# Moving the copy of a tile's attention sums from the next tile's first task to the place directly behind the sums

## The chip, the cores and the metric

The kernel runs on one core of a Trainium2 chip. The metric is device time in microseconds (us) of one execution, as the median of several runs. A core has a matrix engine (PE, with its weight loads PEld), a vector engine (DVE), a scalar engine (ACT), a general engine (POOL) and a queue engine that issues transfers (SP). Each works through its own list of instructions in order, and they wait for each other by semaphores.

## What is computed

The input is x of shape 2 x 2048 x 256 in float32, that is 4096 rows or 32 tiles of 128 rows. Two layers follow each other, each a product of two branches:

```
xn = layernorm(x)
x1 = x  + attention_L0(xn) * silu(experts_L0(xn))     # first layer
xn = layernorm(x1)
out = x1 + block_L1(xn) * silu(two_layer_block(xn))   # block_L1: the main branch
```

attention_L0 has 16 heads with a window of 128 rows, plus a "latent" attention over means of 32 rows, and a sigmoid gate per head that mixes the two. experts_L0 sends every row to one of eight experts. block_L1 is a layer norm, attention in buckets of 64 rows that see their own and the previous bucket, an output projection, and a GELU feed-forward. The two-layer block (local attention with 8 heads, a gated feed-forward, twice) lies between the two and isn't touched here.

For both attentions the part that matters is the same. For a tile n with two blocks of 64 rows: scores, softmax weights without the division, weights times values (the sums), then sums divided by the weights' totals, turned, and multiplied by the output matrix.

## The kernel before, in words

There are three stages in time. The first layer (attention and experts together) takes about the first 980 us, the two-layer block runs from there to about 2490 us, and the main branch runs from there to the end at 3112 us.

**A tile of attention.** Tile n has the runs 2n and 2n+1, one for each block of 64 rows. In the first layer a run has these tasks. `turn(i, half)` transposes two of the four weight tiles on PE (line 151) and copies them out of PSUM (`pt`, line 69 on ACT or line 71 on DVE, in turn). `small(i)` turns the second half, issues the scores of run i+2 (line 114 on PE, then eight masked minima on DVE at line 107 and eight exponentials on ACT at line 136) and then the sums of run i (`total`, 24 matmuls at line 165 into two PSUM banks called `acc`). In the main branch `turn_weights(i)` turns all four weight tiles (line 1502), and `small(i)` issues the scores of run i+2 (lines 1469, 107 and 1489) and the sums of run i (16 matmuls at line 165).

**What follows a tile's second run.** `finish(n)` returns the steps that end tile n. Its first step is `take`: it copies the two `acc` banks into `aT` in SBUF, one copy on DVE (line 71) and one on ACT (line 69), and inverts the weights' totals `zs` on DVE (lines 860 and 861 in the first layer, line 1522 in the main branch). `divide` transposes `aT` on PE (line 188) and multiplies by the inverse totals on DVE (line 192). In the first layer `weigh`, `gate` and `mix` follow (lines 870 to 883, on POOL, DVE and ACT). `back` transposes the result (line 252) and copies it to `oT` on ACT (line 254), and `out` multiplies by the output matrix (line 261) and adds on DVE (line 890 or 1534).

**The order is written out by hand.** `attention(g)` builds a list (a lane) of pairs of a weight and a step for the four tiles of a group. `in_turn` gives each step of a lane a place by the middle of its weight in the lane's sum, stretches the lane over a given part of the group's time, and issues the steps of all lanes in the order of these places. Other lanes are `head(g+1)` (projections of the next group), `experts()`, the sending of rows to the experts (32 indirect transfers at line 547 on POOL) and, in the main branch, `forward(g)` (the feed-forward, lines 1585 to 1619). The step `none` does nothing and only holds a place. All engines keep the order of issue.

In this order tile n-1's `finish` is spread over tile n: `take` comes right after tile n's first task (`first`, the turning of run 2n), `divide` somewhat later, still ahead of `small(2n)`.

**Buffers.** The `acc` banks come from a pool of two. All other PSUM tiles (`s` for products, `tp` for transposes) share six banks. `aT` has two buffers, `zs` three.

Of the kernel before, what the change touches and what calls it, by code (L numbers as in the profile page):

```python
# [14 lines left out]
NT = B * S // P  # L15
# [3 lines left out]
NG = NT // GT  # L19
# [11 lines left out]
def kernel(ctx: ExitStack, tc: tile.TileContext, io: dict, col: dict):  # L31
# [4 lines left out]
    def sb(pool, shape, tag, bufs=None):  # L36
        kw = {} if bufs is None else {"bufs": bufs}
        return pool.tile(list(shape), F32, name=tag, tag=tag, **kw)
# [4 lines left out]
    def bank(tag):  # L43
        return ps.tile([P, 512], F32, name=tag, tag="acc" if tag == "acc" else "b", bufs=2 if tag == "acc" else 6)
# [45 lines left out]
    def in_turn(*lanes):  # L90

        order = []
        for i, (a, b, lane) in enumerate(lanes):
            total, at = sum(w for w, _ in lane), 0.0
            for w, do in lane:
                order.append((a + (b - a) * (at + w / 2) / total, i, len(order), do))
                at += w
        for _, _, _, do in sorted(order, key=lambda x: x[:3]):
            do()
# [279 lines left out]
    with ExitStack() as l0_ctx, tc.manual_schedule(engines=ordered):  # L379
# [264 lines left out]
            return lane  # L644


        groups, values, zss, accs, scores, turns, outs = {}, {}, {}, {}, {}, {}, {}

        def head(g):

# [163 lines left out]
        def latent_out(n):  # L814

            d = outs[n] = {}

            def take():

                d["latT"] = sb(pa, [64, 2, 64], "latT")  # L820
                for v in range(2):
                    h = slice(32 * v, 32 * v + 32)
                    lat = d["latT"][h]
                    acc = accs[n][v][h, 2:4, :].rearrange("p b (e q) -> p b e q", e=2)
                    first, second = (cols[h, col[name] : col[name] + 1] for name in ("first", "second"))
                    nc.scalar.activation(lat, acc[:, :, 0, :], AF.Copy, scale=first)
                    nc.vector.scalar_tensor_tensor(lat, acc[:, :, 1, :], second, lat, ALU.mult, ALU.add)

            def spread():
                mm = bank("s")  # L830
                for blk in range(2):
                    for e in range(2):
                        nc.tensor.matmul(
                            mm[64 * e : 64 * e + 64, blk * P : (blk + 1) * P],
                            lhsT=d["latT"][:, blk, :],
                            rhs=routw[:, e, :],
                            start=True,
                            stop=True,
                        )
                rem = d["rem"] = sb(pa, [P, 16, 16], "rem")  # L840
                nc.vector.tensor_tensor(
                    rem.rearrange("p (b h) d -> p b (h d)", b=2),
                    mm[:, 0 : 2 * P].rearrange("p (b n) -> p b n", b=2),
                    bc(brout, 1, [P, 2, P]),
                    ALU.add,
                )
                d["g2"] = sb(pa, [P, 16, 16], "g2")
                nc.gpsimd.tensor_tensor(d["g2"], rem, bc(gr, 1, [P, 16, 16]), ALU.mult)

            return take, spread  # L850

        def finish(n):

            d = outs[n]

            def take():
                acc = accs.pop(n)
                d["aT"] = sums_out(pa, acc)
                zs = zss[n]
                nc.vector.tensor_scalar(zs, zs, 1e-30, None, ALU.max)  # L860
                nc.vector.reciprocal(zs, zs)

            def divide():
                d["o"] = divided(pa, d["aT"], zss.pop(n))

            lo = lambda: d["o"].rearrange("p b v s d -> p (b v s) d")

            def weigh():
                d["g1"] = sb(pa, [P, 16, 16], "g1")
                nc.gpsimd.tensor_tensor(d["g1"], lo(), bc(gl, 1, [P, 16, 16]), ALU.mult)  # L870
                nc.gpsimd.tensor_tensor(d["g1"], d["g1"], d["g2"], ALU.add)
                nc.gpsimd.tensor_tensor(lo(), lo(), d["rem"], ALU.subtract)

            def gate():
                d["gate"] = sb(pa, [P, 16], "gate")
                nc.vector.tensor_reduce(d["gate"], d["g1"], AX.X, ALU.add)
                nc.scalar.activation(d["gate"], d["gate"], AF.Exp, scale=-1.0)

            def mix():
                nc.vector.tensor_scalar(d["gate"], d["gate"], 1.0, None, ALU.add)  # L880
                nc.vector.reciprocal(d["gate"], d["gate"])
                nc.vector.tensor_tensor(lo(), lo(), bc(d["gate"], 2, [P, 16, 16]), ALU.mult)
                nc.gpsimd.tensor_tensor(lo(), lo(), d["rem"], ALU.add)

            def back():
                d["oT"] = turned_out(pa, d["o"].rearrange("p b v s d -> p b (v s d)"))

            def out():
                s = sb(pa, [P, D], "s")
                nc.vector.tensor_tensor(s, times_out(d["oT"], outw), bout, ALU.add)  # L890
                nc.sync.dma_start(rows_s[:, n, :], s)
                del outs[n]

            return [take, divide, weigh, gate, mix, back, out]

        def attention(g):

            lane = []
            none = lambda: None
            for n in range(GT * g, GT * (g + 1)):  # L900
                take, divide, weigh, gate, mix, back, out = finish(n - 1) if n else [none] * 7
                take_latent, spread = latent_out(n)
                ahead = [none] * 3
                if n + 1 < NT:
                    ahead = [lambda f=f, n=n: f(n + 1) for f in (scale_latent, turn_latent, project_values)]
                def small(i, before):

                    turn(i, 1)
                    for f in before:
                        f()  # L910
                    if i + 2 < 2 * NT:
                        score(i + 2)
                    total(i)

                first, second = (lambda i=i: turn(i, 0) for i in (2 * n, 2 * n + 1))
                latent = [lambda n=n: total_latent(n), take_latent]
                lane += [(1, first), (0.5, take), (1.2, none), (0.8, divide), (0.3, weigh), (0.5, none)]
                lane += [(2.4, lambda n=n, latent=latent: small(2 * n, latent)), (0.3, gate), (1, none), (0.6, spread), (2, none)]
                lane += [(1, second), (0.3, ahead[0]), (0.3, mix), (1.7, none)]
                lane += [(2.4, lambda n=n: small(2 * n + 1, [])), (0.7, none), (0.6, ahead[2]), (0.7, none)]  # L920
                lane += [(0.4, back), (0.7, none), (0.3, ahead[1]), (0.7, none), (0.5, out), (0.5, none)]
            return lane

# [10 lines left out]
        for g in range(NG):  # L934
# [20 lines left out]
                (_, fetch), *rest = gate_head(0)  # L955
                lanes += [(0.3, 0.4, [(1, fetch)]), (0.77, 1, rest)]
            in_turn(*lanes)
        for step in finish(NT - 1):
            step()

    wd = ctx.enter_context(tc.tile_pool(name="wd", bufs=1, side="left"))
# [5 lines left out]
    with tc.tile_pool(name="pd", bufs=2, side="left") as pd, tc.manual_schedule(engines=ordered):  # L967
# [81 lines left out]
        x1s, tiles, scores, turns, accs, outs = {}, {}, {}, {}, {}, {}  # L1049
# [298 lines left out]
        for r in range(NR):  # L1348
            lanes.append((r, r + 1, attention(r)))
            ahead = [prepare(m) for m in range(GT * r + 2, min(GT * r + GT + 2, NM))]  # L1350
# [27 lines left out]
    with tc.tile_pool(name="pc", bufs=2, side="left") as pc, tc.manual_schedule(engines=ordered):  # L1378
# [5 lines left out]
        zero_v = sb(pc, [P, 2, P], "zero_v", 1)  # L1384
        nc.vector.memset(zero_v, 0.0)
        yout = io["out"].rearrange("b (n p) d -> p (b n) d", p=P)
        groups, values, zss, accs, scores, turns, outs = {}, {}, {}, {}, {}, {}, {}

        def head(g):

# [149 lines left out]
        def attention(g):  # L1540

            lane = []
            none = lambda: None
            for n in range(GT * g, GT * (g + 1)):
                take, divide, back, out = finish(n - 1) if n else [none] * 4
                ahead = (lambda n=n: project_values(n + 1)) if n + 1 < NT else none

                def small(i):

                    if i + 2 < 2 * NT:  # L1550
                        score(i + 2)
                    total(i)

                first, second = (lambda i=i: turn_weights(i) for i in (2 * n, 2 * n + 1))
                lane += [(1, first), (0.3, take), (1.2, none), (0.7, divide), (0.6, none)]
                lane += [(1.2, lambda n=n: small(2 * n)), (1.8, none), (0.5, back), (1, none)]
                lane += [(1, second), (2, none)]
                lane += [(1.2, lambda n=n: small(2 * n + 1)), (0.8, none), (0.5, out), (0.8, none), (1, ahead), (0.6, none)]
            return lane

        def forward(g, t0=0, nt=GT):
# [79 lines left out]
        lanes += [(NG - 1.73, NG - 0.6, forward(NG - 3)), (NG - 0.73, NG - 0.25, forward(NG - 2))]  # L1641
        lanes.append((NG - 0.24, NG, forward(NG - 1, 0, 2)))
        in_turn(*lanes)
        in_turn((0, 0.6, [(1, step) for step in finish(NT - 1)]), (0, 1, forward(NG - 1, 2, 1)))
        in_turn((0, 1, forward(NG - 1, 3, 1)))


# [142 lines left out]
```

## Time and profile before

| quantity | value |
|---|---|
| median of 3 runs | 3109.21 us (3105.69 to 3111.13) |
| the profiled execution's own time | 3114.02 us |
| its span, first to last instruction | 3112.2 us |
| granted TensorE clock, mean | 0.947 |
| PE busy | 2757.3 us, 89% |
| DVE busy | 1885.1 us, 61% |
| ACT busy | 1676.9 us, 54% |
| POOL busy | 1064.6 us, 34% |
| instructions | 72624 |
| `aT` copies, DVE and ACT | 64 each, median 378 ns |
| transposes of `aT` (line 188) | 256, median 273 ns |

The page lists busy time for each engine, the span in 40 slices, the chain of work that ended last and the costliest groups of instructions. Other views list one line's or one tile's instructions with what their engine waited for, instructions in order of time, and sums over windows of time. In a row of the timeline the columns are the start and the length in us, engine, line, operation, what it writes and reads, and the count. A matmul in float32 appears twice in the trace for each one in the program. A bracket at the end gives the time that the engine sat idle before the instruction, and who released it.

### The profile page before, as it was taken

How to read it: one execution, taken by the hardware profiler on the slowest of the kernel's cores; microseconds unless marked ns; L12 is line 12 of the kernel's file. 1: busy time of each engine (PE TensorE's matmuls, PEld its weight loads, DVE VectorE, ACT ScalarE, POOL GpSimd, SP SyncE). 2: the span in 40 equal slices, each digit the busy share in tenths (PEclk: the TensorE clock that was granted, in tenths of full speed). 3: DMA queues.
4: the chain of work that ended last, by engine and by line, in shares of the span. 5: the costliest groups of instructions: out<-in, count | busy, mean ns of one | idle time of the engine just before them, and what ended most of it. 6: DMA issues, size and time to landing. Idle time of an engine off the chain costs nothing.

```text
span 3112.2 us, 72624 instructions
## 1 busy us (share of the span) xinstructions
PE 2757.3 (89%) x28250; PEld 1980.8 (64%) x28250; DVE 1885.1 (61%) x6708; ACT 1676.9 (54%) x4598; POOL 1064.6 (34%) x1227
## 2 busy tenths in 40 slices
PE   7776899999994789999999999999998689999997
PEld 4554778877872556665666666666665556666666
DVE  5765555545563777777676676666665375555542
ACT  4544667767771344444544445455553277667662
POOL 1224233323234555454443444443441112222212
PEclk8888999999996899999999999999999899999998
DMA  5001422222212001110000010000000100000000
GB/s 170 13 22 59 142 98 91 94 86 91 98 63 88 26 25 28 28 28 25 15 18 29 15 37 8 8 8 5 5 2 16 57 9 25 22 24 23 15 15 21
DMA packets 88417, 128.63 MB, mean 41 GB/s; under 512 B 8173, under 2 KB 78220, under 8 KB 83084
## 3 DMA queue, kind: packets, MB, share of 16 engines
q1 hardware_dynamic: 85004, 115.60, 11.6%
q0 software_dynamic: 3072, 8.39, 0.8%
q8 instruction: 225, 3.69, 0.5%
q14 instruction: 116, 0.95, 0.1%
HBM read 88.58 MB, written 27.00 MB: 37 GB/s over the span
## 4 chain that ended last, share of the span: by engine, by line
PE 32%; DVE 6%; issue 4%; POOL 4%; ACT 4%; DMA 0%; SPq 0%; POOLq 0%; DVEq 0%; ACTq 0%
PE s L1296 7%; PE s L1612 3%; PE s L1599 3%; PE s L1318 3%; PE s L1086 3%; ACT pr L1489 2%; PE s L1214 2%; POOL inv L1130 1%; PE s L1102 1%; PE acc L1041 1%; POOL scr L1119 1%; PE s L1011 1%; PE tp L151 1%; PE tp L1502 1%; PE s L1469 1%
## 5 line engine op out<-in xcount | busy, mean ns | idle before, releaser
L1031 ACT ACTIVATE pr<-pr,mn 128x192 f32<-128x192 f32 (+2 forms) x512 | 188.6, 439 | 275.8 <-DVE mn L107 271.7
L1130 POOL TENSOR_TENSOR inv<-inv,nhalf 128x16 f32<-128x16 f32 x64 | 188.4, 2944 | 413.6 <-DVE inv L1129 413.6
L107 DVE CUSTOM_DVE_ANT_0 pr<-s,cst 128x128 f32<-128x128 f32 (+2 forms) x1024 | 261.5, 316 | 101.7 <-PE s L1469 81.0
L1296 PE MATMUL s<-h2T,d_w 128*128 128x512 f32 (+2 forms) x792 | 317.0, 555 | 0.6 <-DVE h2T L1286 0.6
L69 ACT COPY pt<-tp 128x384 f32<-128x384 f32 (+3 forms) x320 | 156.3, 495 | 270.9 <-PE tp L151 249.7
L151 PE MATMUL tp<-cst,pr 128*128 128x128 f32 x1488 | 220.3, 285 | 60.5 <-ACT pr L1031 52.0
L136 ACT ACTIVATE pr<-pr,mn 128x192 f32<-128x192 f32 (+2 forms) x512 | 222.9, 436 | 67.4 <-DVE mn L107 67.0
L1489 ACT ACTIVATE pr<-pr,mn 128x128 f32<-128x128 f32 x512 | 198.1, 388 | 112.7 <-DVE mn L107 112.4
L151 PEld LDWEIGHTS tp<-cst,pr 128*128 128x128 f32 x1488 | 180.4, 147 | 102.3 <-ACT pr L1031 57.8
L1119 POOL TENSOR_TENSOR scr<-scr,tab 128x512 f32<-128x512 f32 x128 | 176.8, 1381 | 200.6 <-DVE scr L71 200.5
L1086 PE MATMUL s<-d_wqkv,hT 128*128 128x512 f32 x512 | 243.1, 618 | 0.0
L1296 PEld LDWEIGHTS s<-h2T,d_w 128*128 128x128 f32 x792 | 146.0, 198 | 141.6 <-issue 135.4
L71 DVE COPY pt<-tp 128x384 f32<-128x384 f32 (+3 forms) x320 | 181.3, 567 | 72.0 <-PE tp L151 53.4
L1309 DVE SCALAR_TENSOR_TENSOR u<-s,cols,ge 128x512 f32<-128x512 f32 (+2 forms) x108 | 74.0, 689 | 201.6 <-PE s L1296 130.6
L1318 PE MATMUL s<-d_w,u 128*128 128x256 f32 x768 | 177.9, 382 | 0.0
L165 PE MATMUL acc<-pt,v 64*32 64x128 f32 x4992 | 124.3, 291 | 40.8 <-DVE pt L71 28.5
L1086 PEld LDWEIGHTS s<-d_wqkv,hT 128*128 128x128 f32 x512 | 97.6, 201 | 98.4 <-issue 97.6
L611 PE MATMUL s<-Wo,it 128*128 128x128 f32 x1248 | 158.3, 281 | 1.6 <-ACT it L603 0.8
L1617 POOL TENSOR_TENSOR y<-y,stream 128x256 f32<-128x256 f32 x32 | 23.3, 728 | 391.9 <-DVE y L1616 391.9
L1318 PEld LDWEIGHTS s<-d_w,u 128*128 128x128 f32 x768 | 142.5, 190 | 22.5 <-issue 3.1
L611 PEld LDWEIGHTS s<-Wo,it 128*128 128x128 f32 x1248 | 149.1, 195 | 10.2 <-issue 7.1
L107 DVE CUSTOM_DVE_ANT_0 pr<-s,cst_a 128x192 f32<-128x192 f32 (+2 forms) x512 | 144.0, 347 | 9.3 <-PE s L114 6.9
(271 smaller groups left out, 6416.8 us busy)
## 6 DMA issues: line engine op xcount, KB each, us to landing
w<-in_W1b_dram SPq DMA_DIRECT2D x39, 1028.0 KB
xsort<-zero SPq DMA_DIRECT2D x1, 4992.0 KB
xs<-xsort SPq DMA_DIRECT2D x39, 128.0 KB
ysort<-ys SPq DMA_DIRECT2D x39, 128.0 KB
xn<-in_L_attn_x_dram SPq DMA_DIRECT2D x8, 512.0 KB
rows_s<-s SPq DMA_DIRECT2D x32, 128.0 KB
stream<-in_L_attn_x_dram SPq DMA_DIRECT2D x8, 512.0 KB
sg<-rows_s SPq DMA_DIRECT2D x8, 512.0 KB
```

Of the source, the lines that this page charges most:

```text
L71: nc.vector.tensor_copy(out, in_)
L107: nc.vector.tensor_tensor_reduce(pr, sc, mask, 1.0, CAP, ALU.add, ALU.min, mn)
L136: nc.scalar.activation(w, w, AF.Exp, bias=mn[:, v : v + 1], scale=-1.0, accum_out=zs[:, v, blk, s : s + 1])
L151: nc.tensor.transpose(tp[:, k * P : (k + 1) * P], pr[:, k, :, :].rearrange("p v j -> p (v j)"), ident)
L611: nc.tensor.matmul(mm, lhsT=d["it"][:, ic, :], rhs=late["Wo"][:, ic, h], start=(ic == 0), stop=(ic == FF // P - 1))
L1031: nc.scalar.activation(p, p, AF.Exp, bias=mn[:, w : w + 1], scale=-1.0)
L1086: nc.tensor.matmul(mm, lhsT=heads[r][:, k, t * P : (t + 1) * P], rhs=wqkv_d[l][:, k, j * INNER : (j + 1) * INNER], start=(k == 0), stop=(k ...
L1119: nc.gpsimd.tensor_tensor(d["r2"][:, :, :, 32 * hf : 32 * hf + 32], d["qk"][:, :, :, 32 - 32 * hf : 64 - 32 * hf], bc(d["tab"][:, 2:4, hf, ...
L1130: nc.gpsimd.tensor_tensor(inv.rearrange("p a h -> p (a h)"), inv.rearrange("p a h -> p (a h)"), nhalf, ALU.pow)
L1296: nc.tensor.matmul(mm, lhsT=w1[l][:, k, c, :], rhs=d["h2T"][:, k, 0:w], start=(k == 0), stop=(k == 1))
L1318: nc.tensor.matmul(mm[:, 0:D], lhsT=d["u"][:, c, i * P : (i + 1) * P], rhs=w2[l][:, c, :], start=(c == 0), stop=(c == HC - 1),)
L1489: nc.scalar.activation(w, w, AF.Exp, bias=mn[:, v : v + 1], scale=-1.0, accum_out=zs[:, v, blk, st : st + 1])
```

## The change

In the first layer and in the main branch, `take` of tile n moves from behind `first` of tile n+1 to behind `small(2n+1)` of tile n itself, with the same weight in the lane (0.5 and 0.3). `finish(n)` is therefore called for the tile itself, and its other steps are kept in a dictionary `ends` until the next tile. The last tile's `take` moves likewise from behind the loop into it. The steps of `take` are unchanged: two copies, and one or two small DVE instructions on `zs`. No transfer is among them. Since the weight is put in at a later place of the lane, the steps of a tile between `first` and `small(2n+1)` get places that are 0.5 (of 21.4 for a tile) or 0.3 (of 16.2) earlier against the other lanes.

```diff
-        groups, values, zss, accs, scores, turns, outs = {}, {}, {}, {}, {}, {}, {}
+        groups, values, zss, accs, scores, turns, outs, ends = {}, {}, {}, {}, {}, {}, {}, {}
@@ attention(g) of the first layer
-                take, divide, weigh, gate, mix, back, out = finish(n - 1) if n else [none] * 7
+                divide, weigh, gate, mix, back, out = ends[n - 1] if n else [none] * 6
                 take_latent, spread = latent_out(n)
+                take, *ends[n] = finish(n)
...
-                lane += [(1, first), (0.5, take), (1.2, none), (0.8, divide), (0.3, weigh), (0.5, none)]
+                lane += [(1, first), (1.2, none), (0.8, divide), (0.3, weigh), (0.5, none)]
...
-                lane += [(2.4, lambda n=n: small(2 * n + 1, [])), (0.7, none), (0.6, ahead[2]), (0.7, none)]
+                lane += [(2.4, lambda n=n: small(2 * n + 1, [])), (0.5, take), (0.7, none), (0.6, ahead[2]), (0.7, none)]
...
-        for step in finish(NT - 1):
+        for step in ends[NT - 1]:
             step()
@@ attention(g) of the main branch
-                take, divide, back, out = finish(n - 1) if n else [none] * 4
+                divide, back, out = ends[n - 1] if n else [none] * 3
+                take, *ends[n] = finish(n)
...
-                lane += [(1, first), (0.3, take), (1.2, none), (0.7, divide), (0.6, none)]
+                lane += [(1, first), (1.2, none), (0.7, divide), (0.6, none)]
...
-                lane += [(1.2, lambda n=n: small(2 * n + 1)), (0.8, none), (0.5, out), (0.8, none), (1, ahead), (0.6, none)]
+                lane += [(1.2, lambda n=n: small(2 * n + 1)), (0.3, take), (0.8, none), (0.5, out), (0.8, none), (1, ahead), (0.6, none)]
...
-        in_turn((0, 0.6, [(1, step) for step in finish(NT - 1)]), (0, 1, forward(NG - 1, 2, 1)))
+        in_turn((0, 0.6, [(1, step) for step in ends[NT - 1]]), (0, 1, forward(NG - 1, 2, 1)))
```

## The prediction

> **What bounds the kernel now.** I read the page's busy times first, then the view of line 188 (the transposes that consume the copies), then the timeline around two tiles, then the windows.
>
> ```profile
> PE 2757.3 (89%) x28250; PEld 1980.8 (64%) x28250; DVE 1885.1 (61%) x6708; ACT 1676.9 (54%) x4598; POOL 1064.6 (34%) x1227
> ```
>
> PE is the fullest engine, so a hole on PE is worth asking about. The view of line 188 on PE lists the holes just before the transposes of `aT`:
>
> ```profile
> L188 PE MATMUL tp<-cst,aT x256: 272/273/473, 64.2 to 3080.1; 128*128 128x128 f32 x128
> its engine sat idle before it (us, times) until:
>   DVE aT L71: 28.0, 22
>   DVE zs L860: 24.2, 21
>   ACT aT L69: 8.2, 8
> ```
>
> PE stood still for 28.0 + 24.2 + 8.2 = 60.4 us, 1.9% of the span, until a step of `take` was done. That is the most that closing these holes can give directly. The same view cut by time says where they are: 7.4 us before 230, 3.2 from 230 to 322, 18.6 from 322 to 980 (first layer with experts), and in the main branch 4.1 before 2590, 23.1 from 2590 to 2960, 3.9 after it. The two-layer block between (1510 us) has none and isn't touched.
>
> A tile of the first layer, PE and then DVE:
>
> ```profile
> 701.17 0.38 PE L580 MATMUL tp<-cst,xs 128*128 128x128 f32 x2
> 702.80 0.63 PE L188 MATMUL tp<-cst,aT 128*128 128x128 f32 x4 [1.25 <-DVE zs L860]
> ...
> 718.70 0.94 PE L165 MATMUL acc<-pt,v 64*32 64x128 f32 x48
> ```
>
> ```profile
> 701.38 0.29 DVE L614 TENSOR_TENSOR ys<-s,ys 128x128 f32<-128x128 f32 x1 [1.23 <-PE s L611]
> ...
> 702.26 0.39 DVE L71 COPY aT<-acc 128x256 f32<-128x256 f32 x1
> ...
> 720.75 0.08 DVE L107 DVE_READ_ACCUMULATOR2_ANT mn<- 128x1 f32 x1
> 721.65 0.29 DVE L614 TENSOR_TENSOR ys<-s,ys 128x128 f32<-128x128 f32 x1 [0.82 <-PE s L611]
> ```
>
> The sums to be copied at 702.26 had ended at 689. The copy waited for its place: it stands behind expert work (line 614) that itself waits for PE. The next tile's sums end at 719.64. DVE is done with that run's minima at 720.83 and then idle for 0.82 us. There the copy would run at once.
>
> A pair of tiles of the main branch, PE, then DVE, then ACT:
>
> ```profile
> 2812.90 1.09 PE L1502 MATMUL tp<-cst,pr 128*128 128x128 f32 x8
> 2816.44 0.63 PE L188 MATMUL tp<-cst,aT 128*128 128x128 f32 x4 [2.45 <-DVE aT L71]
> 2832.62 0.41 PE L188 MATMUL tp<-cst,aT 128*128 128x128 f32 x2 [0.88 <-DVE aT L71]
> 2834.33 0.44 PE L188 MATMUL tp<-cst,aT 128*128 128x128 f32 x2 [1.29 <-ACT aT L69]
> ```
>
> ```profile
> 2813.79 0.81 DVE L208 TENSOR_SCALAR q<-s,cols,bqo 128x512 f32<-128x512 f32 x1 [3.48 <-ACT q L207]
> 2815.93 0.36 DVE L71 COPY aT<-acc 128x256 f32<-128x256 f32 x1
> ```
>
> ```profile
> 2833.91 0.36 ACT L69 COPY aT<-acc 128x256 f32<-128x256 f32 x1
> ```
>
> Line 208 holds the DVE copy up until ACT has made `q`; in the next tile the ACT copy is last, behind exponentials and `pt`.
>
> **What the copies cost at the new place.** Nothing is added or removed but waits. Each tile's DVE copy (378 ns), ACT copy (378 ns) and `zs` steps (0.16 + 0.25 us in the first layer, 0.24 us in the main branch) now stand behind the run's minima on DVE and exponentials on ACT. In the order of the changed kernel 46 of the 64 DVE copies and 62 of the ACT copies now wait for PE themselves (none and one before). How long? In the timeline the sums end 0.64 us or more before DVE finishes the run's minima in 61 of 64 tiles, and 2.3 us or more before ACT finishes the exponentials. In one tile of the main branch DVE would wait 0.22 us. The last tile of each stage has no scores behind its sums, so its copies wait for the 24 or 16 matmuls directly, 1.1 us at most, twice. Queued behind are `rv`, `v` and `s` on DVE, which themselves wait for later PE work, and on ACT the copy `oT` in the first layer and `pt` in the main branch. A wait can't gain anything, so its ends are 0 and 0.2 + 2 x 1.1 = 2.4 us in all; I take 0, since in all but three tiles the sums are ready first.
>
> What is late behind them: on ACT in the first layer, `oT` (line 254) by 0.38 us. PE waits for it before line 261 13 times (8.6 us), 6 of them after 322 (3.9 us). There the copy is on the path: 6 x 0.38 = 2.3 us lost. Elsewhere ACT waits for PE first (18 times, 29.8 us before line 254), which hides the 0.38; without that cover it is 31 x 0.38 = 12 us. In the main branch `pt` on ACT ends when it did, since the copy merely changes places with it.
>
> The other steps get places 0.5 of 21.4 or 0.3 of 16.2 earlier. In the changed order `divide` stands ahead of line 580 instead of behind it in some tiles, `spread` (line 833) ahead of line 594, a gate step on POOL ahead of line 584, and one store of `s` on SP moves up past others. Price of one such exchange: up to 0.65 us (line 833's length) either way; I book 1.3 us lost in sum, ends +6 and -6.
>
> **What each stage gives.**
> Before 230: half of the 7.4, 3.7 us; the rest meets the `oT` copy and DVE chains that stay. From 230 to 322: 0, because the path is elsewhere:
>
> ```profile
> 321.79 0.66 PE L580 MATMUL tp<-cst,xs 128*128 128x128 f32 x2 [13.68 <-DMA xs<-xsort]
> ```
>
> PE waits 13.68 us for rows that POOL sends one at a time, about 2.67 us apart from 226 on. Time won on PE meanwhile only lengthens this wait.
> From 322 to 980: PE is busy for 597.7 of 658 us, and ACT's waits are for PE, so closed holes stay closed: 18.6 - 2.3 - 1.3 = 15.0 us.
> Main branch before 2590: 4.1, less 1.0 for the copies of `pt` that become last (that wait is already there three times, 2.3 us): 3.1 us.
> From 2590 to 2960 there are five pairs of 2.45 + 0.88 + 1.29 = 4.62 us (23.1 in all). In the first of a pair, line 188 can follow line 1502 at 2814.0, but the feed-forward's bank is freed by line 208 at about 2814.9 (it moves 0.38 later, behind ACT's copy). Line 1599 then starts at 2815.0 instead of 2816.9: 1.94 us, not 2.45. From there ACT leads: table load 1.28, two GELUs 1.38, table load 1.28, eight exponentials 3.1. In the second of a pair ACT's copy moves ahead of `pt` (0.5 us). Its end comes 1.94 + 0.5 = 2.44 us earlier, and PE still waits for it there for about 2 us. So 5 x 2.44 = 12.2 us, not 23.1.
> After 2960: 3.9 less 0.9 in a tile where line 1585 waits for `h` right after, plus 0.9 at the end, where line 188 slides into a hole of 3.55 us: 3.9 us.
>
> **The clock.** Behind three of the five 2.45 us holes the clock is halved, as in the second of these windows, of one and the same sequence of instructions:
>
> ```profile
> 2669.30:2674.00 4.70, 4.63 (x28) 2.37 (x28) 0.85 (x2) 1.21 (x2) 0.00 (x0) 1.00 0.01 3
> 2742.00:2748.40 6.40, 6.34 (x28) 2.96 (x28) 0.84 (x2) 1.23 (x2) 0.00 (x0) 0.73 0.00 0
> ```
>
> The columns are the window, its length, busy time of PE, PEld, DVE, ACT and POOL, and the granted clock: 0.73 instead of 1.00 costs 1.7 us. [...] By the rows it gets up to 3 x 1.7 = 5.1 us. The row decides, but a hole of 2 us stays in each pair, so I take 2.
>
> Sum: 3.7 + 0 + 15.0 + 3.1 + 12.2 + 3.9 + 2 = 39.9, say 40 us. The profiled execution took 3114.0 us (span 3112.2) and should take 3074. It is 4.8 us above the median of the runs, 3109.2, so the median should be 3069.
>
> **Rivals.**
> *A, as summed: 3069.* Chance 0.63.
> *B, new waits take most of it.* In the pairs ACT leads throughout, and before 322 the sending absorbs all. Left are 10 of the 15 us from 322 on, 3.1 and 3.9 in the main branch and some 3 of the pairs: 20 us, 3089. For it: ACT's busy run from 2820 to 2835 without a hole. Against: ACT waited 3.6 us for line 1599 just before. Chance 0.19.
> *C, everything closes.* All 60.4 and 5 of clock: 3109 - 65 = 3044. Chance 0.07.
> *D, slower.* The copy on ACT ahead of `oT` costs its 0.38 us in each of 31 tiles, and the holes at line 188 only move on to line 165. 3109 + 12 = 3121. It decides once ACT, rather than line 252 on PE, is last before `oT` in most tiles; the 29.8 us that ACT waits there speak against it. Chance 0.05.
> *E, nothing happens.* The copies land, in time, where they were, because other lanes' steps precede them. Against: in the changed order only one or two instructions stand between the minima and the copy. 3109. Chance 0.06.
>
> **How the numbers follow.** A measurement of this kernel can tell about 0.2%, 6 us, from no change. Faster: A, B, C together, 0.89. Same: E, 0.06. Slower: D, 0.05. A's own range is 3055 to 3083 (the reorderings' 6, the clock's 3, the halves taken before 230 and in the pairs). The range given, 3051 to 3094, holds A and B and leaves out C, D and E, 0.18.
>
> **What would show it.** Right: in the profile after, `aT` copies on DVE directly behind line 107, holes before line 188 in the first layer near zero, and in the main branch only ACT's copy as a releaser, about 10 us in all; the wait at line 580 near 320 longer by some 3 us; the middle block unchanged. Wrong: new holes before lines 165, 261 or 1599 of the size of those closed, or PE's clock lower in the first layer.

## The result and the profile after

| quantity | before | after |
|---|---|---|
| median of 4 runs | 3107.74 us (3105.69 to 3111.13) | 3058.88 us (3056.74 to 3061.11) |
| ratio, with its 95% interval | | 0.9839 (0.9826 to 0.9851) |
| the profiled execution's own time | 3114.02 us | 3057.81 us |
| its span | 3112.2 us | 3056.0 us |

The change saves 48.9 us by the medians and 56.2 us by the two profiled executions; the 7 us between them are the distance of the profiled execution of before from its median, 6 us, and 1 us on the other side. The forecast was 3069 us (40 us saved), with a range of 3051 to 3094.

Line numbers from about 901 on are 1 higher in the kernel after, and 2 higher from about 1546 on: line 1469 is 1470, 1502 is 1503, 1522 is 1523, 1599 is 1601, 1612 is 1614. Lines 188, 208 and 261 are where they were.

The page's busy times, kernel after:

```profile
PE 2743.0 (90%) x28250; PEld 1979.2 (65%) x28250; DVE 1884.3 (62%) x6708; ACT 1675.5 (55%) x4598; POOL 1064.8 (35%) x1227
```

DVE, ACT and POOL do what they did. PE is busy 14 us less with the same number of instructions, so a part of the gain must be faster matmuls. The view of line 188, kernel after:

```profile
L188 PE MATMUL tp<-cst,aT x256: 272/273/422, 62.1 to 3020.5; 128*128 128x128 f32 x128
its engine sat idle before it (us, times) until:
  ACT aT L69: 11.3, 11
```

Both rows with DVE as releaser (28.0 and 24.2 us) are gone. What is left is the copy on ACT, 11.3 us where it was 8.2.

A tile of the first layer, kernel after, DVE and then PE:

```profile
676.28 0.41 DVE L71 COPY aT<-acc 128x256 f32<-128x256 f32 x1
```

```profile
685.20 0.60 PE L188 MATMUL tp<-cst,aT 128*128 128x128 f32 x4
```

The copy ends 8.5 us before PE comes to line 188, which starts without a hole.

A pair of tiles of the main branch, kernel after, DVE, PE and ACT:

```profile
2766.33 0.36 DVE L71 COPY aT<-acc 128x256 f32<-128x256 f32 x1
2769.99 0.81 DVE L208 TENSOR_SCALAR q<-s,cols,bqo 128x512 f32<-128x512 f32 x1 [3.30 <-ACT q L207]
```

```profile
2769.76 0.60 PE L188 MATMUL tp<-cst,aT 128*128 128x128 f32 x4
2770.85 3.70 PE L1601 MATMUL s<-h2T,d_w 128*128 128x512 f32 x8 [0.49 <-DVE q L208]
...
2785.63 0.38 PE L188 MATMUL tp<-cst,aT 128*128 128x128 f32 x2
2787.90 0.44 PE L188 MATMUL tp<-cst,aT 128*128 128x128 f32 x2 [1.89 <-ACT aT L69]
...
2802.57 0.44 PE L188 MATMUL tp<-cst,aT 128*128 128x128 f32 x2 [0.22 <-ACT aT L69]
```

```profile
2787.50 0.35 ACT L69 COPY aT<-acc 128x256 f32<-128x256 f32 x1
```

The DVE copy now runs 3.7 us ahead of line 208, which still waits 3.30 us for ACT. The hole of 2.45 us is gone, and 0.49 us of it is back at line 1601, as the prediction had it. In the second tile of the pair the wait is for ACT's copy alone, which runs right behind the eight exponentials. A third tile waits 0.22 us, which the prediction did not have.

Line 580, kernel after:

```profile
310.86 0.66 PE L580 MATMUL tp<-cst,xs 128*128 128x128 f32 x2 [19.50 <-DMA xs<-xsort]
```

The start moved from 321.79 to 310.86, and the wait grew from 13.68 to 19.50 us. The same PE instructions of both traces, laid beside each other, give the gain so far at each point (the time is that of the kernel before):

| point | earlier by | won in the stage | predicted |
|---|---|---|---|
| 320 us, after line 580 | 10.9 us | 10.9 | 3.7 |
| 980 us, end of the first layer | 29.1 us | 18.2 | 15.0 |
| 2435 us, end of the two-layer block | 29.1 us | 0 | 0 |
| 2475 us, start of the main branch | 32.4 us | 3.3 | main branch up |
| 2590 us | 33.3 us | 0.9 | to here: 3.1 |
| 2960 us | 50.1 us | 16.8 | 12.2 + 2 |
| the end | 56.2 us | 6.1 | 3.9 |

The 3.3 us at the start of the main branch may not be the change's: the profiled executions of e9, e11 and e12, told of below, lose as much there against the kernel after, and those of e2 and e7 don't.

### The profile page after: what moved, and what is told of

Same layout as the page of the kernel before. It is cut to its first block, busy times and chain, and to the rows that moved or that the text cites. A ratio compares the mean times of both kernels' runs of the same rounds, so it can differ in the third digit from the quotient of the medians.

```text
span 3056.0 us, 72578 instructions
## 1 busy us (share of the span) xinstructions
PE 2743.0 (90%) x28250; PEld 1979.2 (65%) x28250; DVE 1884.3 (62%) x6708; ACT 1675.5 (55%) x4598; POOL 1064.8 (35%) x1227
## 4 chain that ended last, share of the span: by engine, by line
PE 30%; DVE 6%; issue 6%; POOL 4%; ACT 4%; DMA 0%; SPq 0%; POOLq 0%; DVEq 0%; ACTq 0%
PE s L1297 7%; PE s L1319 3%; PE s L1087 3%; ACT pr L1490 3%; PE s L1614 2%; PE s L1601 2%; PE s L1215 2%; POOL inv L1131 1%; PE s L1103 1%; PE acc L1042 1%; POOL scr L1120 1%; PE s L1012 1%; PE tp L151 1%; PE s L214 1%; PE tp L1066 1%
## 5 line engine op out<-in xcount | busy, mean ns | idle before, releaser
L1310 DVE SCALAR_TENSOR_TENSOR u<-s,cols,ge 128x512 f32<-128x512 f32 (+2 forms) x108 | 73.9, 689 | 199.4 <-PE s L1297 124.2
```

## Experiments

Twelve kernels ran, each timed in five rounds beside the kernel before on the same chip. The theory: the gain comes from the place of the copies in the queues of DVE and ACT, and PE waits for whichever of the two ends last. Rivals: the gain comes from the other steps' earlier places against the other lanes (their places shift because the weight is taken out); one engine's copy explains all; the copies have become free.

| run | median, us | before beside it, us | ratio (95%) |
|---|---|---|---|
| e1_first_only | 3081.76 | 3109.02 | 0.9908 (0.9893 to 0.9923) |
| e2_main_only | 3086.04 | 3109.02 | 0.9933 (0.9919 to 0.9946) |
| e3_shift_only | 3113.72 | 3109.02 | 1.0014 (1.0007 to 1.0021) |
| e4_move_only | 3064.77 | 3109.02 | 0.9862 (0.9846 to 0.9877) |
| e5_dve_moved | 3078.06 | 3112.29 | 0.9890 (0.9875 to 0.9905) |
| e6_act_moved | 3111.95 | 3112.29 | 1.0002 (0.9993 to 1.0010) |
| e7_twice_new | 3078.86 | 3112.29 | 0.9888 (0.9873 to 0.9903) |
| e8_twice_old | 3135.02 | 3112.29 | 1.0074 (1.0060 to 1.0087) |
| e9_main_on_dve | 3042.55 | 3112.49 | 0.9774 (0.9761 to 0.9787) |
| e10_all_on_dve | 3041.60 | 3112.49 | 0.9768 (0.9754 to 0.9782) |
| e11_act_twice | 3074.71 | 3112.49 | 0.9877 (0.9862 to 0.9892) |
| e12_dve_twice | 3063.89 | 3112.49 | 0.9839 (0.9825 to 0.9852) |

Below, a gain or loss is the ratio's distance from 1, or from the 0.9839 of the kernel after, times 3110 us. The interval of each ratio is about 0.0014 to either side, 4 us (half of it for e3 and e6), so a difference between two of the gains is known to some 6 us.

### Which stage: the first layer alone, the main branch alone

The first kernel has only the first layer's lines of the change, the second only the main branch's:

```diff
 e1: -  lane += [(1, first), (0.5, take), (1.2, none), (0.8, divide), (0.3, weigh), (0.5, none)]
     +  lane += [(1, first), (1.2, none), (0.8, divide), (0.3, weigh), (0.5, none)]
     +  ... small(2 * n + 1, []), (0.5, take), (0.7, none) ...
 e2: -  lane += [(1, first), (0.3, take), (1.2, none), (0.7, divide), (0.6, none)]
     +  lane += [(1, first), (1.2, none), (0.7, divide), (0.6, none)]
     +  ... small(2 * n + 1), (0.3, take), (0.8, none) ...
```

> The first layer as changed, the main branch as before. Theory (holes before line 188 close, each stage keeps its own gain): the profile after showed PE 29 us ahead at the end of the first layer, of which I put up to 5 down to differences between executions, so 22 to 29 us off the median of before (ratio 0.991 to 0.993). Rival (only one of the two stages matters): 0 to 5 us, or the whole 49.

> The main branch as changed, the first layer as before. Theory: 22 to 27 us off (ratio 0.991 to 0.993), of which 16 to 17 between the first feed-forward and the last groups, with no window of halved clock there; together with the first-layer-only kernel it adds up to the whole, 49 us, within 4. Rival (only one stage matters): 0 to 5, or 49.

The first layer alone saves 28.6 us, the main branch alone 20.8 us (22 to 27 were expected). The sum, 49.4, is what the whole change saves (50.1), so the stages don't take from each other. The view of line 188 in e2:

```profile
  DVE zs L860: 24.2, 21
  ACT aT L69: 12.9, 13
  DVE aT L71: 3.5, 4
```

All 24.2 us before line 860's inversions are the first layer's and stay, and most of DVE's copies' 28.0 us are gone. In e1 it is the other way about: line 860 is gone, and 24.4 us of DVE's copies and 6.7 of ACT's stay.

### Which cause: the copies' place, or the other steps' places

The third kernel leaves the copies where they were and shifts the other steps as the change does. The fourth moves the copies and shifts nothing else.

```diff
 e3: -  (1, first), (0.5, take), (1.2, none) ...      small(2 * n + 1, []), (0.7, none)
     +  (1, first), (0.25, none), (0, take), (0.95, none) ...      small(2 * n + 1, []), (0.5, none), (0.7, none)
 e4: +  (1, first), (0.5, none), (1.2, none) ...      small(2 * n + 1, []), (0.25, none), (0, take), (0.45, none)
 and in the main branch in the same way, with 0.3 for 0.5
```

> The copies stay where they were before, but their weight in the lane moves as in the change, so that all other steps get the places that they have after it. Theory (the copies' own place makes the gain): within 6 us of before, and the holes before line 188 are back, 50 us or more. Rival (the exchange of other steps makes the gain): 25 us or more off.

> The copies move as in the change, but the weight stays where it was, so that all other steps keep the places of before. Theory: 43 to 52 us off before, within 6 us of the changed kernel, no hole before line 188 but ACT's 11 us. Rival (exchange of other steps): under 25 us off.

The shift alone costs 4.4 us; the move alone saves 42.9, the low end of what was expected. Line 188 in e3, then in e4:

```profile
  DVE aT L71: 43.6, 35
  DVE zs L860: 15.8, 14
  ACT aT L69: 8.4, 7
```

```profile
  ACT aT L69: 10.5, 6
  DVE aT L71: 6.2, 6
```

In e3 the holes add up to 67.8 us, more than the 60.4 before; in e4 to 16.7. So for the whole gain the queue place is the cause, and the rival of the shifted steps falls. (In the stretch before 322 us alone it doesn't; see below.) By the ratios the whole change is 7.2 us better than e4, by the profiled executions it is not (3057.81 and 3058.36 us). DVE's 6.2 us in e4 are a hole of 1.19 us in each of the five pairs, which the change doesn't have, and the pairs' stretch gains 15.0 us there for 16.8; before 2435 us e4's profile is the faster one by 5.7 us. So whether the shift helps in sum once the copies have moved is open.

### Which engine: one half of the step at a time

`take` is split. In e5 DVE's copy and the `zs` steps move and ACT's copy stays; in e6 ACT's copy moves and the rest stays. The other steps shift in both.

```diff
 e5: +  def take():  copy(0, d["aT"][:, 0, :, :], ...);  zs ...      # behind small(2n+1)
     +  def rest():  copy(1, d["aT"][:, 1, :, :], ...)               # behind first of the next tile
 e6: +  def take():  copy(1, d["aT"][:, 1, :, :], ...)
     +  def rest():  copy(0, d["aT"][:, 0, :, :], ...);  zs ...
```

> Only the DVE half of the step moves (its copy and the two or one steps on the weights' totals); the ACT copy stays behind the next tile's first task; all other steps have the places of the changed kernel. Theory (each hole closes as far as its releaser moves): the first layer's holes were released by DVE almost alone, so some 25 us there; in the main branch ACT's copy ends 0.2 us behind DVE's in the short holes, which stay, and the long ones lose about 1.5 us and their halved clock, 12 us: 37 us off before (ratio 0.988), with ACT as the only releaser before line 188. Rival (only both together free the banks and so help): under 8 us.

> Only the ACT copy moves; the DVE half stays behind the next tile's first task. Theory: nothing in the first layer, and in the main branch only the five holes that ACT released last (1.29 us each): 2 to 8 us off before. Rival (the ACT side matters as much): 20 us or more.

DVE's half alone saves 34.2 us, ACT's half alone nothing (0.6 us slower, the interval spans zero; 2 to 8 us were expected), both together 50.1. Line 188 in e5, then in e6:

```profile
  ACT aT L69: 33.4, 38
```

```profile
  DVE aT L71: 46.6, 36
  DVE zs L863: 13.6, 12
  ACT aT L69: 4.1, 5
```

In e5 one row replaces three: where DVE is done early, PE waits for ACT's copy 38 times instead of 8. A hole with two releasers closes only as far as the second. The view of before names only the last releaser of a hole (ACT 8.2 us), so it could not tell how late the other one was. Line 863 of e6 is line 860.

### What a copy costs at each place

Every copy is made twice, writing the same values again: at the new place (e7) and at the old one (e8). Then only ACT's (e11) or only DVE's (e12) at the new place.

```diff
         for v in range(2):
-            copy(v, aT[:, v, :, :], acc[v][:, 0:2, :])
 e7, e8: +   for _ in range(2):
 e11:    +   for _ in range(1 + v):
 e12:    +   for _ in range(2 - v):
         +       copy(v, aT[:, v, :, :], acc[v][:, 0:2, :])
```

> The changed kernel with each of the two copies issued twice, which writes the same values again. Theory (the new place is off the path, save ahead of oT and where ACT leads in the main branch): 2 to 8 us slower than the changed kernel, so 41 to 47 us off before. Rival (the copies cost their length wherever they stand): 64 x 0.38 = 24 us slower than the changed kernel, so 25 us off before.

> The kernel before with each of the two copies issued twice. Theory (the old place is on the path of 51 of 64 tiles): the holes before line 188 grow by 0.38 us each, 15 to 20 us slower than before (ratio 1.005 to 1.0065). Rival (the copies' length doesn't matter at the old place, only what they queue behind): under 4 us slower.

> The changed kernel with ACT's copy alone issued twice. Issuing both twice cost about 15 us where I had expected 2 to 8. Theory (ACT leads in the main branch): ACT's alone costs 8 to 13 of them, so 36 to 41 us off before. Rival (DVE's copy is the dear one): under 4 us, so 45 us off or more.

> The changed kernel with DVE's copy alone issued twice. Theory: 2 to 6 us slower than the changed kernel, through the steps ahead of the sending of rows and through line 208, so 43 to 47 us off before. Rival (DVE's copy is the dear one): 10 us or more, so under 39 us off before.

At the old place the doubled copies cost 23 us, somewhat more than expected: 0.36 us for each of 64 tiles, about the length of one copy (378 ns). They were on the path in nearly every tile, as the holes said. At the new place they cost 15 us (e7), more than expected, so "free at the new place" falls for at least one engine. The single ones tell which: ACT's costs 12 us, DVE's none that can be told from zero. Line 188 stands at 189 in these kernels; e11:

```profile
  ACT aT L69: 15.7, 11
```

It was 11.3 us in the kernel after, and is 11.1 in e12. In e11 line 1601 waits 4.5 us for line 208 where it waited 2.4, since line 208 waits for ACT's `q`. So each of the five pairs pays for ACT's second copy three times, 0.4 us each time: before line 1601 and before line 188 of the two tiles that follow. These are 4.4 + 2.1 = 6.5 us. The profiled execution of e11 is 17.6 us above that of the kernel after: 5 us in the first layer, 3 at the start of the main branch (where e12 is late by the same), 7.4 in the pairs (1.6 of it a stretch at half clock) and about 1 behind them. How much of the 5 is ACT's copy, and how much the variation told of below, was not separated.

### The copy on the other engine

Since DVE's copy costs nothing and ACT's is the last releaser left, both copies go to DVE: in the main branch (e9) or everywhere (e10).

```diff
-    def sums_out(pool, acc):
+    def sums_out(pool, acc, on=(0, 1)):
...
-            copy(v, aT[:, v, :, :], acc[v][:, 0:2, :])
+            copy(on[v], aT[:, v, :, :], acc[v][:, 0:2, :])
...
 e9:  +  d["aT"] = sums_out(pc, accs.pop(n), (0, 0))      # main branch
 e10: +  copy(0, ...) in both stages
```

> The changed kernel, with both copies of a tile on DVE in the main branch. Theory (what is left at the new place is ACT's lead: its copy stands behind eight exponentials, and 11 us of holes before line 188 wait for it): those holes go, and ACT is 0.38 us shorter per tile where it leads, so 5 to 12 us less than the changed kernel, 54 to 61 us off before (ratio 0.980 to 0.983). Rival (the rest of ACT's chain gates the same matmuls anyway): within 4 us of the changed kernel.

> The changed kernel with both copies on DVE in both stages. Theory: as with the main branch alone, and in the first layer ACT's oT comes 0.38 us earlier at the eight waits before line 261 (3 us), against a DVE that is longer by 0.39 us where it feeds the sending of rows (2 us): within 4 us of the kernel with the main branch alone. Rival (DVE leads in the first layer as well): 8 us or more slower than that one.

Both beat both kernels: 3042.55 and 3041.60 us, 20 us less than the kernel after by the ratios (15 us by the profiled executions), where 5 to 12 were expected. Line 188 of e9 has no releaser at all. The pair of tiles in e9, PE and then DVE:

```profile
2760.01 0.60 PE L188 MATMUL tp<-cst,aT 128*128 128x128 f32 x4
2760.84 3.70 PE L1601 MATMUL s<-h2T,d_w 128*128 128x512 f32 x8 [0.23 <-DVE q L208]
...
2775.62 0.60 PE L188 MATMUL tp<-cst,aT 128*128 128x128 f32 x4
```

```profile
2756.58 0.68 DVE L71 COPY aT<-acc 128x256 f32<-128x256 f32 x2
2759.98 0.81 DVE L208 TENSOR_SCALAR q<-s,cols,bqo 128x512 f32<-128x512 f32 x1 [2.71 <-ACT q L207]
```

The hole of 1.89 us is closed and that at line 1601 went from 0.49 to 0.23. DVE's wait before line 208 fell from 3.30 to 2.71 us: the second copy fills a stretch in which DVE stood still. Against the kernel after, PE wins 2.8 us in each of the first four pairs and 2.5 in the fifth, 13.7 of the profile's 15 us: the holes of 1.89, 0.22 and 0.26 us, and line 188 no longer cut in two. The kernel after splits the two copies over both engines; here the split costs 20 us by the ratios, because ACT is the engine that is late at this place (11.3 us of holes before line 188 wait for its copy). In the first layer the choice makes no difference (3041.60 us in e10, 3042.55 in e9).

## Why the prediction was right, point by point

The sum said 40 us; the medians gave 48.9 and the two profiled executions 56.2. The mechanism held and the size was short. By the profiles the misses are the stretch before 322 us (7.2 us more than booked), the clock (4.8 more), 322 to 980 us (3.2 more), what follows 2960 us (2.2 more), the five pairs (2.6 less), and the main branch before 2590 us (1.1 more, or 2.2 less if the 3.3 us at its start are not the change's).

**The mechanism** was right: the copies had waited for their place behind other lanes' steps (e3 against e4), the holes before line 188 closed in the first layer, and in the main branch ACT's copy alone is left. "About 10 us in all" came out as 11.3.

**The cost of waiting at the new place**, taken as 0 from ends of 0 to 2.4 us, held: in e12 even a doubled DVE copy costs nothing that can be told. But the waits of the last tiles were not "1.1 us at most": ACT stands idle 10.19 us before its copy at 929.8 and DVE 3.64 us at 3012.4. The first costs nothing, since ACT had stood idle there before the change too, 12.45 us at 960.6 until line 252 on PE was done.

**`oT` on ACT**, 6 x 0.38 = 2.3 us. In the view of line 261, kernel after:

```profile
  ACT oT L254: 11.1, 17
```

The wait grew by 2.5 us, from 8.6, as booked.

**Before 322 us** the size was off: 10.9 us for 3.7. Part is no effect of the change. Before 320 us executions of one order differ by several us: e2 has the first layer of the kernel before and reaches line 580 at 317.9 instead of 321.8. Against e1 (308.3), which ran beside e2 and has only the first layer changed, the gain is 9.6 us. PE comes to line 489 (ranks of the rows) 3.6 us earlier. That is near the predicted 3.7, but before and e2 differ by 4.1 us at this point, so the agreement shows little. The other 5.9 us come behind it, where executions of one order agree within 1 us. This is the step of the sum that failed: "From 230 to 322: 0, because the path is elsewhere", and nothing at all for what lies between the ranks and the sending. The path there runs through DVE and POOL. The times from the start of line 489, in us:

| run | its product with `ones` | first send of rows | line 870 | line 580 |
|---|---|---|---|---|
| before | 4.3 | 16.1 | 27.7 | 124.2 |
| e2 (first layer as before) | 4.3 | 16.1 | 27.9 | 124.3 |
| e3 (other steps shifted alone) | 1.6 | 12.6 | 22.7 | 122.1 |
| e4 (copies moved alone) | 3.8 | 15.1 | 25.4 | 120.3 |
| after | 2.6 | 13.6 | 21.9 | 119.2 |
| e1 (first layer as after) | 2.6 | 13.6 | 22.1 | 118.4 |

Inside line 489 PE waits for DVE's `ones` (line 483), 3.7 us before and 1.9 after. And POOL, before and then after, between two sends of rows:

```profile
225.25 0.73 POOL L870 TENSOR_TENSOR g<-o,rows_a 128x256 f32<-128x256 f32 x1 [4.97 <-DVE o L192]
```

```profile
213.56 0.72 POOL L870 TENSOR_TENSOR g<-o,rows_a 128x256 f32<-128x256 f32 x1 [1.71 <-DVE o L192]
```

On POOL the next send comes behind line 870 (at 227.63 us, and at 215.92 after the change), and before line 870 POOL stood idle for 4.97 us, after the change for 1.71, until a product (line 192) was there that comes behind line 188 and the late copy. The prediction had looked only at line 188 for victims of the copy. But the copies are the smaller part here. Up to line 870 the change gains 5.7 us; e3, which leaves the copies in place, gains 5.0, and e4, which moves nothing else, 2.2. So most of it comes with the other steps' earlier places, for which the prediction had booked 1.3 us lost. In the sends that follow, e3 gives 2.9 us back; why was not traced.

**322 to 980 us**: 15.0 predicted, 18.2 measured. The holes were 18.6, less 2.3 for `oT` is 16.3. The 1.9 us beyond, against 1.3 us that were booked as lost by reorderings (with ends of 6 either way), are within what executions differ by: e2, with the old order, is 3.3 us faster in this stretch than the profiled execution of before, and e1 against e2 gains 14.3.

**The five pairs** gave 9.6 us, not 12.2, and the clock 6.8, not 2: two errors that cancel in part, by luck. Each pair is 2.36 us ahead after its second tile (predicted 2.44), and loses 0.43 in the third, where line 188 is cut in two by the wait of 0.22 us for ACT's copy. Before, that tile had no hole.

**The clock.** The prediction found three stretches at half clock and expected a hole of 2 us to keep some of them. There were four in the five pairs, three behind a hole of 2.45 us and this one:

```profile
2613.70:2617.10 3.40, 3.40 (x6) 1.34 (x5) 0.50 (x2) 1.11 (x2) 0.00 (x0) 0.50 0.00 0
```

All are gone (the granted clock, third from the right, for the pairs of the kernel after):

```profile
2555.00:2915.00 360.00, 338.59 (x3426) 230.72 (x3425) 208.09 (x987) 257.34 (x840) 81.64 (x130) 1.00 0.07 22
```

Four times 1.7 us are 6.8. Holes of 2.45 us were followed by half clock three times of five in the kernel before and five times of five in e3 (last section), so this size is that of two executions. Behind 2960 us, 6.8 us more stand at half clock in the profile of before than in that of after, which can be worth up to 3.4 us and so can cover the 2.2 us won there beyond the forecast.

**The rivals.** B (20 us, new waits take most of it) would have needed the pairs and the early part to give nearly nothing; they gave 9.6 and about 10. It was right in that ACT leads there: e9 takes that away and gains 20 us more. C (everything closes) came out short by what ACT's copy and `oT` hold back. D (slower, by ACT's copy ahead of `oT`) is there at 2.5 us, not 12. E falls with the profile after: on ACT 60 of the 64 copies stand directly behind a run's exponentials.

## What to carry to other kernels

A copy out of PSUM that has to wait for its turn in an engine's list, and not for its data, belongs directly behind its producer's run, and all halves of it must move: the consumer waits for the last one (34 us with one half, 0 with the other, 50 with both). Look for its victims beyond PE's own hole: here POOL's queue of transfers stood behind a product of that copy (4.97 us of idle time before line 870, 1.71 after). Such a change also shifts the steps around it, so time the move alone and the shift alone: before the sending the shift gave 5.0 us and the move 2.2, in the whole the shift cost 4 and the move saved 43. Then ask which of the engines is late at the new place, by doubling the copy on one at a time, and give the copy to the other: that was worth 20 us more.

## What was not expected of the hardware

**The clock and the place of a hole.** In the five pairs of the main branch the same sequence of instructions comes with holes of different length. With 1.89 us (kernel after) none of five was followed by half clock; with 2.29 us (e11) one of five; with 2.45 us three of five in the kernel before and five of five in e3. So in these places the length alone doesn't tell. The holes also differ in where they lie. In the traces of the kernels before and after, all 44 and all 41 stretches at half clock start on one grid for each trace, with steps of 3.413 us (to 1 ns). Here are cells of this grid in the kernel before, two around a hole of 2.45 us that was spared, then two around one that was not:

```profile
2664.89:2668.31 3.41, 2.03 (x24) 1.62 (x23) 1.59 (x4) 3.06 (x10) 0.00 (x0) 1.00 0.00 0
2668.31:2671.72 3.41, 2.35 (x9) 1.42 (x10) 1.76 (x5) 0.87 (x1) 0.00 (x0) 1.00 0.00 0
2739.99:2743.40 3.41, 1.34 (x7) 0.90 (x8) 2.59 (x8) 1.85 (x3) 0.00 (x0) 1.00 0.00 0
2743.40:2746.81 3.41, 3.41 (x6) 1.35 (x5) 0.18 (x1) 0.69 (x1) 0.00 (x0) 0.50 0.00 0
```

The first hole is divided between two cells, 1.38 and 1.07 us, and the clock stays. Of the second, 2.07 us fall into one cell (PE is busy for 1.34 of 3.41), and the next cell is at half clock. In these two traces ten holes of 1.88 us or more lie before line 188 of the pairs. Three of them, all in the kernel before, put 2.07, 2.24 and 2.37 us into one cell, and each was followed by half clock; the other seven put at most 1.88 us into one, and none was. So each of these holes of 2.45 us was hit or spared as 2.07 us or more of it, or 1.38 us or less, fell into one cell; what sets the clock was not shown. The fourth stretch of the kernel before fits: holes of 0.88 and 1.30 us lie in one cell. Over the whole of the two traces this holds less strictly: of 61 cells at full clock with 2.0 us or more of idle PE, 54 are followed by half clock; of 1463 with less than 1.0, 9 are.

**Executions differ most before 320 us.** With the first layer's order of before, line 580 started at 321.8 (before) and 317.9 (e2); with that of the change at 310.9 (after), 308.3 (e1) and 308.4 (e9). From 322 to 980 us before and e2 differ by another 3.3 us. A difference of 4 us in either stretch between two profiles isn't evidence.

**What stays open:** why the doubled DVE copy costs nothing also in the first layer, where DVE's chains precede PE; whether the 7 us between e4 and the kernel after are the shift's; and why, behind line 870, the sends take longer in e3.
